# Perceiver layer on one core: half tiles shared by a pair of batches, probabilities left undivided with their inverses turned in DRAM, scores on other banks right behind the logits, softmax in parts

## The chip, the cores and the metric

The kernel runs on one core of one Trainium2 chip. The metric is the device time of one execution in microseconds. All data are float32.

## The reference

There are 32 batches with 64 latents x (128 features) and a context of 1,601 rows of 128 features. A mask selects for each batch at most 400 rows at the end of its context. Three residual blocks follow each other:

```python
# cross attention: 16 heads of 64; keys and values are the selected context rows and the 64 latents
q = ln(x) @ Wq * scale; k, v = split([ln(ctx), ln(x)] @ Wkv)
x = x + layernorm(softmax(mask(q @ k.T)) @ v @ Wout)
# self attention over the 64 latents: 16 heads of 8, a slope bias on the distance
x = x + softmax(q @ k.T / sqrt(8) + slopes * dist) @ v @ Wo + bo
# feed-forward: SiLU gate, 128 -> 352 -> 128, activations and weights rounded to 8 bits,
# with one scale over the maximum of all batches
x = x + ffn(layernorm(x))
```

## The kernel before, in words

The batches are sorted on the chip by how many context rows they need, and each place in the sorted order has a fixed cap (`CAPS`, line 26). If the caps do not hold, a switch (line 910) takes one of two wider versions; with these inputs the first, called narrow, runs. Two batches are worked on as a pair (t, u), u = 0 or 1: place t with place 31 - t (`batch`, line 182). A batch has 64 + cap columns of keys: one tile of 128 rows that holds the latents of one of the two and 64 context rows, then nt = (cap - 64) // 128 full tiles, then a rest. With the caps before, there is no rest.

The weights are folded ahead: a_sb is Wq times Wk for each head and b_sb is Wv times Wout, so a query has 128 features and is multiplied with the normalised context itself, whose rows also serve as values.

A pair has 8 steps, one for each couple c of heads. All 16 pairs make 128 steps. For each step and batch:

- `logits` (lines 553 to 585): one matmul of the queries with the turned context into bank_s (L568), at most 512 columns; VectorE adds the mask and takes the minimum of the negated logits (L571); ScalarE takes the exponential and sums it (L576). VectorE then inverts the sums (L582) and multiplies the probabilities with them (L585).
- `turned` (lines 587 to 619): two steps later TensorE transposes the probabilities tile by tile into bank_t (L604, L614), and ScalarE copies them out (L607, L615).
- `attend` (lines 621 to 640): after every second step TensorE multiplies context rows by turned probabilities for four heads, 256 columns a tile, into bank_m (L632), and VectorE copies the result out (L637).

After a pair's steps `project` (L663) applies b_sb over 16 heads, the layer norm follows, and the self-attention of the pair: `self_T` (L689), `self_qkv` (L700 to L722), `self_softmax` (scores L738, bias addition L750, maximum L754, subtraction L755, exponential L759), `self_pT`, `self_values` (L788), `self_out` (L804). Before a pair's steps `load` brings context rows and mask (L445 to L455) into one of three buffers, `prepare` normalises them (moments L494, then L502, L224, L225), `keys_T` turns them (L243), and `queries` (L544) multiplies latents by a_sb.

There are eight PSUM banks: two bank_s, three bank_t, three bank_m. The program is written as a list of steps: `at(step, f, ...)` enters a function under a step, and the last loop runs the logits of a step, then what stands under it. `chain` (lines 832 to 837) gives the steps after a pair's end at which the parts of its self-attention stand. A scheduler then orders the instructions of each engine; each engine and each DMA queue runs its own in order. All loads in the loop go through SP's queue.

After the loop the feed-forward part (lines 915 to 1029) needs the maximum over all batches first.

Of the kernel before, what the change touches and what calls it, by code (L numbers as in the profile page):

```python
# [25 lines left out]
CAPS = [448] * 9 + [320] * 8 + [192] * 7 + [64] * 8  # L26
# [11 lines left out]
def perceiver_layer(  # L38
# [16 lines left out]
    small = ctx.enter_context(tc.tile_pool(name="small", bufs=4))  # L55
    ps_s = ctx.enter_context(tc.tile_pool(name="ps_s", bufs=2, space=PSUM))
# [125 lines left out]
    def batch(t, u, engine=mybir.EngineType.SP, reorder=True, order=order):  # L182

        r = t if u == 0 else B - 1 - t
        _, (b,) = nc.values_load_multi_w_load_instructions(
            order[:, r : r + 1], engines=[engine], min_val=0, max_val=B - 1,
            skip_runtime_bounds_check_because="five bits of an integer", bass_reorder=reorder,
        )
        return b
# [196 lines left out]
    def attention(actx, name, caps):  # L386
# [4 lines left out]

        keep = actx.enter_context(tc.tile_pool(name=f"keep{name}", bufs=1))
# [3 lines left out]
        def cap(t, u):  # L396
            return caps[t if u == 0 else B - 1 - t]

        def shape(t, u):

            nt, rest = divmod(cap(t, u) - SL, P)
            return nt, rest, [P] * (1 + nt) + [rest] * (rest > 0), SL + cap(t, u)

        n_max = [max(len(shape(t, u)[2]) for t in range(NP)) for u in range(2)]
        k_max = [max(shape(t, u)[3] for t in range(NP)) for u in range(2)]
# [17 lines left out]
        for u in range(2):  # L423
            for x_ in xns[u]:
                nc.gpsimd.memset(x_[lat[u], 0, :], 0.0)
                if not narrow:
                    nc.gpsimd.memset(x_[:, n_max[u] - 1, :], 0.0)
            for a_ in addends[u]:
                nc.gpsimd.memset(a_[:, lat[u]], 0.0)
# [5 lines left out]
        masks, lns, lnTs, xTs, qTs, oTs, probs, pTs = {}, {}, {}, {}, {}, {}, {}, {}  # L435

        def load(t, u):
            r = xns[u][t % NX]
            nt, rest, _, _ = shape(t, u)
            first = S2 - cap(t, u)  # L440
            b = first_pair[u] if t == 0 else batch(t, u)
            if t and narrow:
                load_x(t, u, b)
            rows = context[bass.ds(b, 1)].rearrange("b s d -> (b s) d")
            nc.sync.dma_start(out=r[tok[u], 0, :], in_=rows[first : first + SL])  # L445
            lo = first + SL
            if nt:
                nc.sync.dma_start(
                    out=r[:, 1 : 1 + nt, :],
                    in_=rows[lo : lo + nt * P].rearrange("(p n) d -> p n d", n=nt),  # L450
                )
            if rest:
                nc.sync.dma_start(out=r[:rest, 1 + nt, :], in_=rows[S2 - rest :])
            m = two.tile([P, cap(t, u)], U8, tag=f"mask{u}", name=f"mask{t}_{u}")
            nc.sync.dma_start(  # L455
                out=m,
                in_=mask[bass.ds(b, 1)].rearrange("b s -> (b s)")[first:].partition_broadcast(P),
            )
            masks[t, u] = m
# [26 lines left out]
        def prepare(t, u):  # L486

            nt, rest, tiles, sk = shape(t, u)
            n_all = len(tiles)
# [11 lines left out]
            for n in range(n_all):  # L501
# [8 lines left out]
            nc.gpsimd.tensor_scalar(  # L510
                ad[:, tok[u]], m[:, :SL], BIG, -BIG, ALU.mult, ALU.add
            )
            if nt:
                nc.gpsimd.tensor_scalar(
                    ad[:, P : P + nt * P].rearrange("q (n p) -> q n p", p=P),
                    m[:, lo:hi].rearrange("q (p n) -> q n p", n=nt),
                    BIG, -BIG, ALU.mult, ALU.add,
                )
            if rest:
                nc.gpsimd.tensor_scalar(  # L520
                    ad[:, P + nt * P : sk], m[:, hi:], BIG, -BIG, ALU.mult, ALU.add
                )

        def keys_T(t, u):
            nt, rest, _, sk = shape(t, u)
            xn = xns[u][t % NX]
            xT = two.tile(
                [P, k_max[u]], FP, tag=f"xT{u}", name=f"xT{t}_{u}", bufs=2 if narrow else 1
            )
            view = xT[:, : (1 + nt) * P].rearrange("p (n c) -> p n c", c=P)  # L530
            for n in range(0, 1 + nt, 4):
                e = min(n + 4, 1 + nt)
                transposed(view[:, n:e, :], [xn[:, j, :] for j in range(n, e)], nc.scalar.copy)
            if rest:
                transposed(xT[:, (1 + nt) * P :].unsqueeze(1), [xn[:rest, 1 + nt, :]])
            xTs[t, u] = xT
# [16 lines left out]
        def logits(t, c, us):  # L553

            den = small.tile([P, len(us)], FP, tag=f"den{name}", name="den")
            for i, u in enumerate(us):
                sk = shape(t, u)[3]
                w = qTs[t][:, u, 2 * c : 2 * c + 2, :].rearrange("p h i -> p (h i)")
                s = two.tile(
                    [P, k_max[u]], FP, tag=f"s{u}" if narrow else "s", name=f"s{t}_{u}_{c}",  # L560
                    bufs=4 if narrow else 2,
                )[:, :sk]
# [3 lines left out]
                for j, (k, e) in enumerate(pieces):  # L566
                    ps = bank_s()
                    nc.tensor.matmul(  # L568
                        ps[:, : e - k], lhsT=w, rhs=xTs[t, u][:, k:e], start=True, stop=True
                    )  # L570
                    nc.vector.tensor_tensor_reduce(  # L571
                        out=s[:, k:e], in0=ps[:, : e - k], in1=addends[u][t % NA][:, k:e],
# [5 lines left out]
                    accum_out=den[:, i : i + 1],  # L578
                )
                probs[t, u, c] = s  # L580
            rden = small.tile([P, len(us)], FP, tag=f"rden{name}", name="rden")
            nc.vector.reciprocal(rden, den)  # L582
            for i, u in enumerate(us):
                s = probs[t, u, c]
                nc.vector.tensor_scalar_mul(s, s, rden[:, i : i + 1])  # L585

        def turned(t, c, u):

            nt, rest, tiles, _ = shape(t, u)
            n_all = len(tiles)  # L590
# [19 lines left out]
            for n in range(0, 1 + nt, 4):  # L610
                e = min(n + 4, 1 + nt)
                bt = bank_t().rearrange("p (j c) -> p j c", c=P)
                for j in range(n, e):
                    nc.tensor.transpose(bt[:, j - n, :], s[:, j * P : (j + 1) * P], ident)  # L614
                nc.scalar.copy(pT[:, n:e, odd, :], bt[:, : e - n, :])  # L615
            if rest:
                bt = bank_t()
                nc.tensor.transpose(bt[:rest, :P], s[:, (1 + nt) * P :], ident)
                evacuate(pT[:rest, 1 + nt, odd, :], bt[:rest, :P])

        def attend(t, c, u):
# [5 lines left out]
            pT = pTs.pop((t, u, c))  # L627
            po = bank_m()
            xn = xns[u][t % NX]
            tiles = shape(t, u)[2]  # L630
            for n, k in enumerate(tiles):
                nc.tensor.matmul(  # L632
                    po[:, : 2 * P], lhsT=xn[:k, n, :],
                    rhs=pT[:k, n].rearrange("p o c -> p (o c)"),
                    start=(n == 0), stop=(n == len(tiles) - 1),
                )
            nc.vector.tensor_copy(  # L637
                oTs[t][:, 2 * c : 2 * c + 4, u, :],
                po[:, : 2 * P].rearrange("p (h i) -> p h i", i=SL),
            )  # L640
# [17 lines left out]
        def project(t, part, parts=2):  # L658
# [8 lines left out]
            if part < parts - 1:  # L667
                return
            oTs.pop(t)
# [61 lines left out]
        def self_softmax(t):  # L731
            q, kx = own[t]

            ps = [bank_s(), bank_t(), bank_m(), bank_m()]
# [10 lines left out]
            stat = small.tile([P, H], FP, tag="stat", name="stat")  # L745
            for g in range(2):
                hs = slice(g * 8, g * 8 + 8)
                for r in (2 * g, 2 * g + 1):
                    hr = slice(4 * r, 4 * r + 4)
                    nc.vector.tensor_tensor(  # L750
                        p[:, hr], ps[r][:, : 4 * SL].rearrange("p (h k) -> p h k", k=SL),
                        bias[:, hr], ALU.add,
                    )
                nc.vector.tensor_reduce(stat[:, hs], p[:, hs], AX.X, ALU.max)  # L754
                nc.vector.tensor_tensor(  # L755
                    p[:, hs], p[:, hs],
                    stat[:, hs].unsqueeze(2).to_broadcast([P, 8, SL]), ALU.subtract,
                )
                nc.scalar.activation(p[:, hs], p[:, hs], AF.Exp)  # L759
            own[t] = p  # L760

# [40 lines left out]
        def self_out(t):  # L802
            po = bank_m()
            nc.tensor.matmul(po[:, :D], lhsT=own.pop(t), rhs=swT[:, 3, :], start=True, stop=True)  # L804
            nc.vector.tensor_tensor(x1[:, t, :], po[:, :D], x1[:, t, :], ALU.add)
            norm1(x3[:, t, :], x1[:, t, :])
# [23 lines left out]
        for t in range(NP):  # L830
            s0, e = CH * t, CH * (t + 1)
            if not narrow:
                chain = (4, 5, 9, 10, 12, 16, 17, 18, 19)
            elif t < NP - 2:
                chain = (4, 5, 7, 8, 10, 13, 14, 15, 16)
            else:
                chain = (None, None, 4, 5, 6, 8, 8, 9, 10)
# [6 lines left out]
            if t == NP - 1:  # L844
                for k in range(3):
                    at(e + chain[2], ffn_turn, k)
            for k, (f, *more) in zip(
                chain[2:],
                (
                    (self_T,), (self_qkv,), (self_softmax,), (self_pT, 0), (self_pT, 1),  # L850
                    (self_values,), (self_out,),
# [48 lines left out]
        for i in range(max(later) + 1):  # L900
            if i < len(steps):
                logits(*steps[i])
            for f, args in later.get(i, ()):
# [161 lines left out]
```

## Time and profile before

| | us |
|---|---|
| median of 3 runs (lowest, highest) | 691.11 (690.61, 691.83) |
| the profiled execution | 692.31 |
| its span | 690.3 |
| mean granted TensorE clock | 0.961 |
| PE busy / VectorE / ScalarE / GpSimd | 620.7 / 518.7 / 409.8 / 130.0 |
| PE idle before L568, released by VectorE's L750 / L571, whole span | 11.3 / 9.0 |
| start of the first and last logits record | 33.2 / 593.2 |

The profile is one execution, taken by the hardware. L568 is line 568 of the kernel. PE is TensorE's matmuls, PEld its weight loads, DVE VectorE, ACT ScalarE, POOL GpSimd, SP the engine that issues most DMAs. A row of a group gives line, engine, operation, output <- inputs, shape and count, then busy time and the mean ns of one, then the idle time of the engine just before the group and what released it. A row of a window gives the stretch, its length, the busy time (and instructions) of PE, PEld, DVE, ACT and POOL, the granted clock, the share of DMA time and GB/s. A row of a wait gives total us, times, longest. A row of the chain gives start, length and what the chain of waits followed there. A DMA row ends with the median time from issue to landing.

### The profile page before, as it was taken

The page shows a single profiled execution, that of the slowest core. Times are in us where ns is not written, and L with a number is a line of the kernel's source. Part 1 is how long each engine was busy: PE and PEld are TensorE (multiplying, and loading weights), DVE is VectorE, ACT ScalarE, POOL GpSimd, SP SyncE. Part 2 cuts the span into 40 slices and gives each one's busy share as a digit, 9 for nine tenths or more (in the row PEclk, how much of TensorE's full clock was granted, in tenths as well). Part 3 has the DMA queues.
Part 4 walks back from the last instruction along what each step waited for, and adds up shares of the span by engine and source line. Part 5 has one row for each costly group of instructions (what it writes and reads, how often), then busy time and mean ns, then how long its engine had stood idle before and what let it go on. Part 6 is the DMA issues. An engine that isn't in the chain of part 4 may idle for free.

```text
span 690.3 us, 14206 instructions
## 1 busy us (share of the span) xinstructions
PE 620.7 (90%) x4798; PEld 496.9 (72%) x4798; DVE 518.7 (75%) x1992; ACT 409.8 (59%) x1096; POOL 130.0 (19%) x273
## 2 busy tenths in 40 slices
PE   4598999999998989898999999999999999954975
PEld 3576878777786868686878888888887886843335
DVE  4487777787868797878778888888888778644673
ACT  2386667666675766675766767676766566512441
POOL 1338320211111112121111212020202000010002
PEclk9599999999999999999999999999999999975988
DMA  4520100000001010100000010000000000000002
GB/s 103 118 56 0 25 1 24 2 24 1 24 2 23 2 30 1 24 1 20 5 11 14 11 15 8 18 7 19 5 24 1 1 1 1 1 1 3 1 0 62
DMA packets 20580, 11.98 MB, mean 17 GB/s; under 512 B 7748, under 2 KB 20036, under 8 KB 20500
## 3 DMA queue, kind: packets, MB, share of 16 engines
q1 hardware_dynamic: 19476, 10.02, 6.4%
q10 hardware_dynamic: 864, 0.82, 0.4%
q8 instruction: 40, 0.66, 0.4%
q14 instruction: 40, 0.33, 0.2%
q0 software_dynamic: 160, 0.16, 0.1%
HBM read 9.94 MB, written 1.05 MB: 16 GB/s over the span
## 4 chain that ended last, share of the span: by engine, by line
PE 49%; DVE 26%; ACT 8%; POOL 5%; issue 5%; DMA 2%; SPq 0%; POOLq 0%; DVEq 0%; ACTq 0%
PE bank_m L632 11%; PE bank_s L568 10%; PE bank_m L663 6%; PE bank_m L544 5%; ACT s L576 5%; DVE s L571 5%; POOL rstd L469 5%; DVE s L585 5%; PE bank_t L614 4%; PE bank_s L971 3%; PE bank_t L243 3%; DVE oT L637 2%; PE bank_m L998 2%; PE bank_t L604 2%; PE bank_m L788 1%
## 5 line engine op out<-in xcount | busy, mean ns | idle before, releaser
L576 ACT ACTIVATE s<-s,low 128x512 f32<-128x512 f32 (+3 forms) x256 | 143.8, 563 | 100.7 <-DVE low L571 87.5
L568 PE MATMUL bank_s<-xT,qT 128*128 128x512 f32 (+3 forms) x512 | 170.6, 449 | 20.6 <-DVE p L750 11.3
L632 PE MATMUL bank_m<-pT,xn 128*128 128x256 f32 x656 | 166.6, 381 | 1.6 <-ACT pT L615 1.4
L568 PEld LDWEIGHTS bank_s<-xT,qT 128*128 128x128 f32 x512 | 88.5, 194 | 77.8 <-DVE p L750 21.5
L469 POOL TENSOR_TENSOR rstd<-rstd,mhalf 128x1 f32<-128x1 f32 (+2 forms) x96 | 61.1, 638 | 411.7 <-DVE rstd L465 387.3
L632 PEld LDWEIGHTS bank_m<-pT,xn 128*128 128x128 f32 x656 | 118.2, 190 | 18.8 <-ACT pT L615 3.4
L571 DVE CUSTOM_DVE_ANT_0 s<-bank_s,ad 128x512 f32<-128x512 f32 (+3 forms) x256 | 121.0, 486 | 8.7 <-PE bank_s L568 7.9
L615 ACT COPY pT<-bank_t 128x512 f32<-128x512 f32 (+1 forms) x136 | 70.4, 523 | 51.5 <-PE bank_t L614 51.3
L585 DVE TENSOR_SCALAR s<-s,rden 128x512 f32<-128x512 f32 (+3 forms) x256 | 89.6, 391 | 2.0
L614 PE MATMUL bank_t<-ident,s 128*128 128x128 f32 x480 | 75.3, 273 | 0.0
L544 PE MATMUL bank_m<-lnT,a_sb 128*128 128x128 f32 x512 | 70.8, 284 | 0.4 <-ACT lnT L244 0.4
L614 PEld LDWEIGHTS bank_t<-ident,s 128*128 128x128 f32 x480 | 60.6, 141 | 13.6 <-issue 1.0
L544 PEld LDWEIGHTS bank_m<-lnT,a_sb 128*128 128x128 f32 x512 | 65.4, 201 | 0.7 <-ACT lnT L244 0.7
L663 PE MATMUL bank_m<-b_sb,oT 128*128 128x128 f32 x512 | 63.3, 276 | 0.5 <-DVE oT L637 0.5
L663 PEld LDWEIGHTS bank_m<-b_sb,oT 128*128 128x128 f32 x512 | 60.0, 192 | 1.7 <-DVE oT L637 1.3
L637 DVE COPY oT<-bank_m 128x256 f32<-128x256 f32 x128 | 53.2, 415 | 10.5 <-PE bank_m L632 10.2
L502 ACT ACTIVATE xn<-xn,shift,rstd 128x128 f32<-128x128 f32 x82 | 36.6, 490 | 25.5 <-DVE shift L498 25.4
L576 ACT ACTIVATION_READ_ACCUMULATOR s<-s,low 128x1 f32 x256 | 48.4, 189 | 0.0
L548 ACT COPY qT<-bank_m 128x512 f32<-128x512 f32 x64 | 37.4, 584 | 16.2 <-PE bank_m L544 15.8
L582 DVE RECIPROCAL rden<-den 128x2 f32<-128x2 f32 x128 | 20.4, 159 | 30.2 <-ACT s L576 29.4
L604 PE MATMUL bank_t<-ident,s 128*128 128x128 f32 x176 | 29.0, 273 | 0.0
L607 ACT COPY pT<-bank_t 128x256 f32<-128x256 f32 (+1 forms) x60 | 28.0, 466 | 0.0
(179 smaller groups left out, 853.5 us busy)
## 6 DMA issues: line engine op xcount, KB each, us to landing
xn<-in_ctx_dram SPq DMA_DIRECT2D x9, 192.0 KB, 2.4
x<-in_x_dram SPq DMA_DIRECT2D x32, 32.0 KB, 2.3
xn<-in_ctx_dram SPq DMA_DIRECT2D x32, 32.0 KB, 2.0
xn<-in_ctx_dram SPq DMA_DIRECT2D x8, 128.0 KB, 2.0
out_dram<-y SPq DMA_DIRECT2D x18, 32.0 KB, 1.9
wk_sb<-in_L_xattn_Wkv_dram ACTq DMA_DIRECT2D x1, 512.0 KB, 4.2
wq_sb<-in_L_xattn_Wq_dram SPq DMA_DIRECT2D x1, 512.0 KB, 5.1
wv_sb<-in_L_xattn_Wkv_dram SPq DMA_DIRECT2D x1, 512.0 KB, 5.3
```

Source lines behind the costliest of these rows:

```text
L469: nc.gpsimd.tensor_tensor(rstd, rstd, mhalf[:, :n], ALU.pow)
L544: nc.tensor.matmul(pm[:, j * P : (j + 1) * P], lhsT=a_sb[:, h4 + j, :], rhs=lnTs[t], start=True, stop=True,)
L568: nc.tensor.matmul(ps[:, : e - k], lhsT=w, rhs=xTs[t, u][:, k:e], start=True, stop=True)
L571: nc.vector.tensor_tensor_reduce(out=s[:, k:e], in0=ps[:, : e - k], in1=addends[u][t % NA][:, k:e], scale=-1.0, scalar=3e38 if j == 0 else ...
L576: nc.scalar.activation(s, s, AF.Exp, bias=low[:, len(pieces) - 1 :], scale=-1.0, accum_out=den[:, i : i + 1],)
L585: nc.vector.tensor_scalar_mul(s, s, rden[:, i : i + 1])
L604: nc.tensor.transpose(bt[:, n, o, :], s[:, n * P : (n + 1) * P], ident)
L614: nc.tensor.transpose(bt[:, j - n, :], s[:, j * P : (j + 1) * P], ident)
L615: nc.scalar.copy(pT[:, n:e, odd, :], bt[:, : e - n, :])
L632: nc.tensor.matmul(po[:, : 2 * P], lhsT=xn[:k, n, :], rhs=pT[:k, n].rearrange("p o c -> p (o c)"), start=(n == 0), stop=(n == len(tiles) - 1),
L637: nc.vector.tensor_copy(oTs[t][:, 2 * c : 2 * c + 4, u, :], po[:, : 2 * P].rearrange("p (h i) -> p h i", i=SL),)
L663: nc.tensor.matmul(pm[:, :D], lhsT=oT[:, h].rearrange("p u i -> p (u i)"), rhs=b_sb[:, h, :], start=(h == 0), stop=(h == H - 1),)
```

## The change

1. **Caps and pairs.** The caps come in steps of 64 and are tighter; the pairs are a written list. A rest is now 0 or 64, the same for both of a pair, and the rests of both lie in one tile: rows 0 to 63 are batch 0's, 64 to 127 batch 1's. The probabilities of both batches lie next to each other, so that this tile is turned by one transpose; its attend matmul is done once for each batch, on half the rows.
2. **Undivided probabilities.** The multiplication L585 goes. The sums of two steps and both batches are inverted together (4 columns). SP writes them, turned, to a small tile in DRAM, and reads that back as one row of 512 values for all 128 partitions. The copy L637 becomes a product with that row.
3. **Scores.** `self_softmax` is split into `self_scores` (the matmuls, and the bias additions) and two halves of the softmax at their own steps. The scores take two bank_t and two bank_m instead of one bank_s, one bank_t and two bank_m, and stand first under their step, right behind the logits.
4. **Norms** that stood inside `project` and `self_out` are functions with steps of their own.

```diff
-CAPS = [448] * 9 + [320] * 8 + [192] * 7 + [64] * 8
+CAPS = [448] * 4 + [384] * 5 + [320] * 2 + [256] * 6 + [192] * 6 + [128] + [64] * 8
+PAIRS = [
+    (17, 31), (4, 15), (0, 24), (5, 14), (18, 30), (6, 13), (1, 25), (19, 22),
+    (7, 12), (2, 26), (16, 23), (8, 11), (3, 27), (20, 21), (9, 28), (10, 29),
+]
...
+    dram = ctx.enter_context(tc.tile_pool(name="dram", bufs=4, space=bass.MemoryType.DRAM))
...
-        r = t if u == 0 else B - 1 - t
+        r = PAIRS[t][u]
...
         def logits(t, c, us):
...
+            odd, n_us = c % 2, len(us)
+            if not odd:
+                sums[t, us[0]] = small.tile([P, 2 * n_us], FP, tag=f"den{name}", name="den")
+            den = sums[t, us[0]]
+            both = two.tile(
+                [P, s_max], FP, tag="s", name=f"s{t}_{us[0]}_{c}", bufs=4 if narrow else 2
+            )
...
-            rden = small.tile([P, len(us)], FP, tag=f"rden{name}", name="rden")
-            nc.vector.reciprocal(rden, den)
-            for i, u in enumerate(us):
-                s = probs[t, u, c]
-                nc.vector.tensor_scalar_mul(s, s, rden[:, i : i + 1])
+            if odd:
+                nc.vector.reciprocal(den, den)
+                line = dram.tile([2 * n_us, P], FP, tag=f"line{name}", name="line")
+                nc.sync.dma_start(out=line.rearrange("j p -> p j"), in_=den)
+                rden = two.tile(
+                    [P, 2 * n_us * P], FP, tag="rden", name=f"rden{t}_{us[0]}_{c}",
+                    bufs=3 if narrow else 2,
+                )
+                nc.sync.dma_start(
+                    out=rden, in_=line.rearrange("j p -> (j p)").partition_broadcast(P)
+                )
+                view = rden.rearrange("d (o u h i) -> d u o h i", h=2, o=2, u=n_us)
+                for i, u in enumerate(us):
+                    sums[t, u, c - 1] = view[:, i]
...
         def attend(t, c, u):
...
-            nc.vector.tensor_copy(
-                oTs[t][:, 2 * c : 2 * c + 4, u, :],
-                po[:, : 2 * P].rearrange("p (h i) -> p h i", i=SL),
-            )
+            if rest and narrow and u == 0:
+                return
+            both = (0, 1) if rest and narrow else (u,)
+            if rest:
+                for v in both:
+                    i, n, on = rest_of(t, v)
+                    nc.tensor.matmul(
+                        open_[v][:, : 2 * P], lhsT=xns[i][t % NX][on, n, :],
+                        rhs=pTs[t, i, c][on, n].rearrange("p o c -> p (o c)"),
+                        start=False, stop=True,
+                    )
+            for v in both:
+                nc.vector.tensor_tensor(
+                    oTs[t][:, 2 * c : 2 * c + 4, v, :].rearrange("p (o h) i -> p o h i", o=2),
+                    open_.pop(v)[:, : 2 * P].rearrange("p (o h i) -> p o h i", o=2, h=2),
+                    sums.pop((t, v, c)), ALU.mult,
+                )
...
-        def self_softmax(t):
+        def self_scores(t):
...
-            ps = [bank_s(), bank_t(), bank_m(), bank_m()]
+            ps = [bank_t(), bank_t(), bank_m(), bank_m()]
...
-                chain = (4, 5, 7, 8, 10, 13, 14, 15, 16)
+                chain = (5, 5, 6, 7, 8, 10, 11, 12, 13, 14, 15, 16, 17)
...
-                chain = (None, None, 4, 5, 6, 8, 8, 9, 10)
+                chain = (None, None, 3, 4, 5, 6, 6, 6, 8, 8, 9, 10, 10)
...
-            for f, args in later.get(i, ()):
+            for f, args in sorted(later.get(i, ()), key=lambda x: x[0] is not self_scores):
                 f(*args)
```

## The prediction

> **What bounds the kernel now.** I read the page's shares first, then the slices, then the busy time of a long stretch, then who waited for whom on PE in that stretch, then the chain that ended last.
>
> ```profile
> PE 620.7 (90%) x4798; PEld 496.9 (72%) x4798; DVE 518.7 (75%) x1992; ACT 409.8 (59%) x1096; POOL 130.0 (19%) x273
> ...
> PEclk9599999999999999999999999999999999975988
> ...
> 50.00:590.00 540.00, 517.57 (x4101) 423.09 (x4100) 431.97 (x1718) 353.69 (x979) 108.58 (x211) 1.00 0.05 11
> ```
>
> The third line is the pair loop: 540 us long, PE busy 517.6 of them at a granted clock of 1.00, DVE 432.0, ACT 353.7. So PE is the bound there and has 22.4 us of idle; the other 150 us of the span are set-up, the tail of the attention and the feed-forward part, which the change leaves alone. The waits of PE in the same stretch name the idle:
>
> ```profile
> PE bank_s L568 <- DVE p L750: 11.3, 12, 1.3
> PE bank_s L568 <- DVE low L571: 8.5, 9, 1.8
> PE bank_m L632 <- ACT pT L615: 1.4, 4, 0.4
> ```
>
> The logits' bank is held by the self-attention's scores (first line), or the logits run ahead of VectorE (second). Whether PE is really full or only looks so is told by the chain of waits, where PE stands uncovered piece after piece:
>
> ```profile
> 327.54 0.87 PE bank_m L632 x4
> 328.41 1.29 PE bank_s L568 x4
> 329.70 0.86 PE bank_m L632 x4
> 330.56 0.44 PE bank_t L614 x4
> 331.00 1.79 PE bank_m L663 x16
> ```
>
> An fp32 matmul leaves two records, a transpose one. Columns per piece: L568 is 2 records of 512 and 2 of 256, 1,536 columns in 1.29 us; L632 is 4 x 256 = 1,024 in 0.86; L614 4 x 128 in 0.44. All give 0.84 to 0.86 ns a column. That is the price I use for PE work: PE streams, and only columns or waits taken away shorten the loop.
>
> **The change part by part.**
>
> *Half tiles and new pairs.* The caps sum to 8,448 before and 7,680 after; with 64 latents for each of 32 batches, 10,496 columns against 9,728, or 82 tiles of 128 against 76. The instruction order of the changed kernel has the same 256 logits matmuls, with 77,824 columns where there were 83,968: 6,144 fewer, two records each, 12,288. Probability transposes go from 656 to 608 (48 x 128 = 6,144 columns), key transposes from 82 to 76 (768). Together 19,200 columns x 0.84 = **-16.1 us** on the bounding engine. The attend matmuls stay 328 of 256 columns: a shared tile is multiplied twice, by 64 rows each.
>
> *Those 48 half matmuls* (24 neighbouring couples, on rows 0-63 and 64-127) may run side by side. The nearest row is the scores, four row groups:
>
> ```profile
> 321.58 0.43 PE L738 MATMUL bank_m<-kx,q 32*64 32x256 f32 x2
> 321.85 0.38 PE L738 MATMUL bank_m<-kx,q 32*64 32x256 f32 x2
> 322.19 0.33 PE L243 MATMUL bank_t<-ident,ln 128*128 128x128 f32 x1
> ```
>
> There 16 records of 256 columns start within 0.30 us and the next transpose 0.62 us after the first; one after the other they would take 16 x 0.215 = 3.4 us. So tiles do overlap. The Trainium skill (TensorEngine Tiling (Array Packing), Key Properties) says against it that changing the tiling mode drains the engine. Four records cost 0.86 us in sequence; side by side 0.43, plus a drain, for which the scores leave 0.62 - 0.43 = 0.19 us. By the overlap alone 24 x 0.43 = 10 us are won, with the drain 24 x 0.24 = 6, and without any overlap the drain loses 24 x 0.19 = 5. I take **-3**, ends -10 and +5.
>
> *Undivided probabilities.* This takes VectorE work away:
>
> ```profile
> L585 DVE TENSOR_SCALAR s<-s,rden 128x512 f32<-128x512 f32 x72 | 35.6, 495 | 0.9
> L637 DVE COPY oT<-bank_m 128x256 f32<-128x256 f32 x128 | 53.2, 415 | 10.5 <-PE bank_m L632 10.2
> L750 DVE TENSOR_TENSOR p<-bank_m,bias 128x256 f32<-128x256 f32 x32 | 13.2, 413 | 0.0
> ```
>
> All four forms of L585 are 89.6 us; 64 reciprocals of 128 go (10.2); the copy of 415 ns becomes a product of a PSUM bank and an SBUF tile of the same size, which L750 does in 413 ns: nothing. L571 costs (676-278)/384 = 1.04 ns a column, x 6,144 = 6.4. VectorE loses about 106 us plus 4 for six tiles of normalisation, so it falls from 518.7 us of the span to some 409. ScalarE loses 5.4 in the exponentials (0.87 ns a column) and about 7 in the copies. None of this is on PE, so it is worth only what it takes out of PE's waits: of the 8.5 us behind L571 I take 3.5 away (ends 0 and 8.5).
>
> *Scores on other banks.* The logits no longer share a bank with the scores, and the four additions come before any maximum. The 11.3 us go. What is late next: the scores now hold two of three bank_t and two of three bank_m until four additions at some 0.33 us are done. In PE's new order about 2 us of attend and logits work lie between the scores and the next instruction that needs a held bank, against about 1.3 us of additions plus what VectorE has in front. I leave 3 us (about 0.2 us x 16; ends 0 and 16). Net **-8** here, **-3.5** above. Cutting the softmax into parts adds no instruction.
>
> *The inverses through DRAM.* Added on SP's queue: 64 times a write of 512 single fp32 elements, and 64 reads of 256 KB that wait for it. Nothing before looks like that write. Nearest rows, issue to landing:
>
> ```profile
> xn<-in_ctx_dram SPq DMA_DIRECT2D x9, 192.0 KB, 2.4
> mask<-in_mask_BxS_bk_dram SPq DMA_DIRECT2D x9, 56.0 KB, 3.0
> sbk_c<-in_L_attn_bk_dram SPq DMA_DIRECT2D x1, 0.5 KB, 3.1
> clip<-in_L_ffn_clip_x_dram SPq DMA_DIRECT2D x1, 0.5 KB, 3.6
> ```
>
> The sbk_c row is 128 elements of 4 bytes (its twin sbq_c took 4.5, but in the set-up, where the DMA engines were 60% busy against 5% in the loop). If 512 cost no more, the write takes 3.1; if every further 128 elements add the 1.1 us by which 128 short rows lie above a 64-row load (2.0), it takes 3.1 + 3 x 1.1 = 6.4. The Trainium skill (DMA: Bandwidth & Descriptors, Rules for kernel authors) speaks against this part: a strided last dimension becomes one descriptor per element; and the page's fixed cost of about 2 us is mostly the receipt of the write, longest for HBM. By the page alone an estimate is 2 us plus something; by the rows 3.1 to 6.4. I take 4.5. The read is near the 192 KB row: 3. With two issues of about 0.5 us, inverse to landing is 4.5 + 0.5 + 3 + 0.3 = **8.3 us**.
>
> Who waits: the product on VectorE, and behind it the logits' L571 and so PE. In the changed order the product stands three or four steps behind its reciprocal in all but three of 64 cases. 128 steps in some 525 us are 4.1 us each, so three are 12.3. For the lightest pairs (384 columns, two of 16) I estimate 5 x 384 x 0.84 ns plus about 1.4 us of shared work = 3.0 us a step, 9.1 for three. It is covered, barely in those. Cost zero, and if the cover is gone, each us missing costs up to 64 us.
>
> SP is moved past too. Each write-read couple blocks it for 4.5 + 0.5 us, and the loads of the pair after next queue between:
>
> ```profile
> SPq L445 <- PE bank_m L632: 386.1, 25, 30.4
> ```
>
> Before, SP spent 386 us waiting for a free context buffer, so there is time; but the loads now start some us later and VectorE's moments of that pair wait for them (3.2 us before). VectorE would be idle for over a third of the loop ((432 - 108) / 525 busy), so I count nothing of that, ends 0 and 12.
>
> *Head and tail.* The first pair has 3 tiles where it had 5: **-1**. The last pair's final product waits for two transfers: 8.3 us after the last reciprocal, where before the last copy came 10.8 us after it (598.2 to 608.9), and the work between shrinks by some 2 to 3 us: **+1** (ends 0 and 5).
>
> Sum: -16.1 - 3 - 8 - 3.5 - 1 + 1 = -30.6. The profiled execution took 692.31 us (span 690.3 and 2.0 around it), so 661.7; the median of the runs is 1.2 lower, so **660.5**.
>
> **The rivals.**
>
> 1. *PE work and waits shrink as summed* (chance 0.64): 660.5, from 648 (L571's waits, the drain and the held banks all at their good ends) to 671.
>
> 2. *The transfers are just late* (0.20): the write lands at about 6 us, light steps and loads behind it hold VectorE by about 2 us in a third of 64 cases, or the held banks cost their full 13 more. 15 us of the gain are lost: 675. For: three steps are only 12 us. Against: VectorE has slack, and two bank_s banks lie between it and PE.
>
> 3. *SP's queue becomes the bound* (0.12), slower than before: write, wait, read and loads go in order. One period is the write's landing L, 0.5 for the read's issue and about 0.9 for a quarter of a pair's loads. The loop before is 557 us, or 8.7 per period of 64, so it decides from L = 7.3 us; at 7.5 the loop is 64 x 8.9 = 570 and the execution about 705. For: no row shows 512 small writes. Against: the rows end at 6.4.
>
> 4. *Nothing is left of it* (0.04): 691, when the held banks and late loads give back some 30 us.
>
> 0.2% of 691, 1.4 us, is about what a measurement of this kernel can tell from no change. Faster: 0.64 + 0.19 + 0.01; within: 0.03; slower: 0.13. The range reaches from 648 to rival 2's far side, 684.
>
> **What would show it.** PE busy should be about 601, L568's columns 155,648, and L585 gone. PE's waits for p L750's successor should be near 3 us. The write's landing time is the number that decides: below 6 us the first case holds; above 7.3 the third, with VectorE idle before the product, released by a DMA. If the half matmuls' records do not overlap, 3 to 8 us are missing.

## The result, and the profile after

The changed kernel takes **890.92 us** (median of 4 runs, 880.99 to 891.43), the kernel before 691.40 beside it (4 runs): ratio 1.285, 95% interval 1.276 to 1.294. The prediction, 660.5 us and faster, was wrong, and 890.92 lies above its range (648 to 684). The profiled execution took 891.43 us, its span is 889.8.

From the page: busy time, the granted clock in 40 slices, and the DMA issues with the median from issue to landing at the end of the row.

```profile
PE 669.6 (75%) x4744; PEld 522.2 (59%) x4744; DVE 436.4 (49%) x1666; ACT 398.5 (45%) x1070; POOL 128.4 (14%) x287
...
PEclk8777788989889898979899898979797898886697
...
rden<-line SPq DMA_DIRECT2D x64, 256.0 KB, 4.6
xn<-in_ctx_dram SPq DMA_DIRECT2D x44, 32.0 KB, 3.3
line<-den SPq DMA_DIRECT2D x64, 2.0 KB, 9.7
```

VectorE's busy time falls by 82 us (518.7 to 436.4), yet PE, the bounding engine, is busy for longer than before and idle for a quarter of the span. The row `line<-den`, the write of the inverses, had been taken at 4.5 us and lands in 9.7. The chain of waits follows the same transfer:

```profile
PE 34%; DMA 31%; DVE 7%; SPq 3%; issue 2%; ACT 2%; POOL 1%; DVEq 0%; ACTq 0%; POOLq 0%
```

Now the loop, from the first to the last logits record: first before, then after (columns as explained ahead of the prediction).

```profile
33.20:593.20 560.00, 537.08 (x4226) 436.99 (x4226) 447.22 (x1789) 368.08 (x1018) 113.90 (x221) 1.00 0.05 13
```

```profile
32.60:779.70 747.10, 582.83 (x4181) 460.81 (x4180) 366.21 (x1470) 357.25 (x994) 113.14 (x233) 0.89 0.25 31
```

The loop holds 187 of the span's 199.5 us of loss; the tail behind it takes 110.1 us where it took 97.1. In the loop PE idle rises from 23 to 164 us (747.1 - 582.8), and PE busy rises by 46 although there is less to stream, at a granted clock of 0.89. Who waits, in the kernel after (SP over the whole span, the others from 50 to 800 us; total us, times, longest):

```profile
SPq L635 <- DMA line<-den: 555.0, 64, 11.3
...
DVE st L522 <- DMA xn<-in_ctx_dram: 131.0, 21, 10.4
DVE oT L712 <- DMA rden<-line: 78.8, 20, 7.7
...
PE bank_s L612 <- DVE low L615: 108.5, 23, 10.1
PE bank_m L695 <- DVE oT L712: 18.4, 7, 6.2
```

SP stands 555 us before the read (L635) until the write has landed. VectorE waits in two places: at the first moments of new context rows (L522), and at the product (L712). PE waits for VectorE's L615 behind either. One such stretch, first on SP's queue:

```profile
322.15 0.39 SPq L630 DMA_DIRECT2D line<-den  x1
332.58 0.32 SPq L635 DMA_DIRECT2D rden<-line  x1
333.17 0.47 SPq L473 DMA_DIRECT2D xn<-in_ctx_dram  x1
...
336.65 0.53 SPq L630 DMA_DIRECT2D line<-den  x1
```

then on VectorE, and on PE (the bracket is the idle time before the instruction and its releaser):

```profile
337.60 0.59 DVE L522 BATCH_NORM_STATS2 st<-xn 128x6 f32<-128x128 f32 x2 [8.29 <-DMA xn<-in_ctx_dram]
```

```profile
339.31 2.50 PE L612 MATMUL bank_s<-xT,qT 128*128 128x512 f32 x4 [5.03 <-DVE low L615]
...
353.75 1.25 PE L612 MATMUL bank_s<-xT,qT 128*128 128x512 f32 x4
```

The read waits 10 us for the write, the context load behind it goes out only at 333.17, VectorE sits idle for 8.29 us for those rows, and PE behind it for 5.03. The logits that follow stream at half speed: 2.50 us at a granted clock of 0.50 (339.31 to 341.81) for what takes 1.25 us at 1.00 from 353.75. So one late transfer is paid twice on PE. The Trainium skill (TensorE: Matmul & The Clock Gate, HAM oscillation) has the rule: idle gaps of PE above about 3.4 us throttle the array again. This stretch, with its gap of 5.03 us, agrees; the last section has one that does not.

### The profile page after: what moved, and what is told of

It reads as the page before. It is cut to its first block, busy times and chain, and to the rows that moved or that the text cites. A ratio compares the mean times of both kernels' runs of the same rounds, so it can differ in the third digit from the quotient of the medians.

```text
span 889.8 us, 14107 instructions
## 1 busy us (share of the span) xinstructions
PE 669.6 (75%) x4744; PEld 522.2 (59%) x4744; DVE 436.4 (49%) x1666; ACT 398.5 (45%) x1070; POOL 128.4 (14%) x287
## 4 chain that ended last, share of the span: by engine, by line
PE 34%; DMA 31%; DVE 7%; SPq 3%; issue 2%; ACT 2%; POOL 1%; DVEq 0%; ACTq 0%; POOLq 0%
DMA line<-den 18%; PE bank_s L612 7%; DMA rden<-line 6%; PE bank_m L695 6%; DMA xn<-in_ctx_dram 4%; PE bank_m L740 4%; PE bank_m L580 3%; PE bank_s L1056 2%; PE bank_t L669 2%; DMA mask<-in_mask_BxS_bk_dram 2%; PE bank_t L249 2%; PE bank_m L1083 1%; DVE s L615 1%; PE bank_t L659 1%; PE bank_m L869 1%
## 5 line engine op out<-in xcount | busy, mean ns | idle before, releaser
L612 PE MATMUL bank_s<-xT,qT 128*128 128x128 f32 (+6 forms) x512 | 178.1, 474 | 110.6 <-DVE low L615 110.5
L620 ACT ACTIVATE s<-s,low 128x128 f32<-128x128 f32 (+6 forms) x256 | 138.1, 541 | 202.3 <-DVE low L615 156.7
L498 POOL TENSOR_TENSOR rstd<-rstd,mhalf 128x1 f32<-128x1 f32 (+3 forms) x96 | 59.0, 622 | 570.9 <-DVE rstd L494 489.7
L695 PEld LDWEIGHTS bank_m<-pT,xn 128*128 128x128 f32 x560 | 108.7, 206 | 51.5 <-DVE oT L712 15.1
L615 DVE CUSTOM_DVE_ANT_0 s<-bank_s,ad 128x128 f32<-128x128 f32 (+6 forms) x256 | 111.6, 465 | 26.1 <-PE bank_s L612 22.8
L712 DVE TENSOR_TENSOR oT<-bank_m,rden 128x256 f32<-128x256 f32 x128 | 52.3, 417 | 96.0 <-DMA rden<-line 84.0
L522 DVE BATCH_NORM_STATS2 st<-xn 128x6 f32<-128x128 f32 x76 | 20.1, 278 | 134.6 <-DMA xn<-in_ctx_dram 134.0
L740 PE MATMUL bank_m<-b_sb,oT 128*128 128x128 f32 x512 | 66.0, 289 | 15.5 <-ACT qT L584 10.1
L580 PEld LDWEIGHTS bank_m<-lnT,a_sb 128*128 128x128 f32 x512 | 68.4, 207 | 11.9 <-DVE ws L363 3.8
L740 PEld LDWEIGHTS bank_m<-b_sb,oT 128*128 128x128 f32 x512 | 63.8, 205 | 18.3 <-ACT qT L584 10.5
L681 ACT COPY pT<-bank_t 128x512 f32<-128x512 f32 (+1 forms) x96 | 52.4, 546 | 23.3 <-PE bank_t L669 13.9
L669 PEld LDWEIGHTS bank_t<-ident,s 128*128 128x128 f32 x312 | 41.0, 150 | 18.3 <-issue 10.1
L841 ACT ACTIVATE p<-p 128x512 f32<-128x512 f32 x32 | 20.0, 629 | 60.7 <-DVE p L838 60.6
L662 ACT COPY pT<-bank_t 128x512 f32<-128x512 f32 (+1 forms) x80 | 37.4, 484 | 1.5 <-PE bank_t L659 1.5
```

The costliest lines, as they stand in the source:

```text
L498: nc.gpsimd.tensor_tensor(rstd, rstd, mhalf[:, :n], ALU.pow)
L580: nc.tensor.matmul(pm[:, j * P : (j + 1) * P], lhsT=a_sb[:, h4 + j, :], rhs=lnTs[t], start=True, stop=True,)
L612: nc.tensor.matmul(ps[:, : e - k], lhsT=w, rhs=xTs[t, u][:, lo + k : lo + e], start=True, stop=True)
L615: nc.vector.tensor_tensor_reduce(out=s[:, k:e], in0=ps[:, : e - k], in1=addends[u][t % NA][:, lo + k : lo + e], scale=-1.0, scalar=3e38 if ...
L620: nc.scalar.activation(s, s, AF.Exp, bias=low[:, len(pieces) - 1 :], scale=-1.0, accum_out=den[:, odd * n_us + i : odd * n_us + i + 1],)
L662: nc.scalar.copy(pT[:, :n_all], bt)
```

## The experiments

Theory S at the start: SP's queue, blocked for the write's landing once per period, paces the loop. Its rivals: the latency from inverse to landed read (some 15 us: 9.7 for the write, 4.6 for the read, two issues) is longer than the three steps it has (L), and the pairs or the scores also cost time.

**Part 2 undone** (`e1_divided`): parts 1, 3 and 4 stay.

```diff
-            if odd:
-                nc.vector.reciprocal(den, den)
...
+            nc.vector.reciprocal(rden, den)
+            for i, s in enumerate(parts):
+                nc.vector.tensor_scalar_mul(s, s, rden[:, i : i + 1])
...
-                nc.vector.tensor_tensor(
+                nc.vector.tensor_copy(
```

> The changed kernel with only its second part undone: probabilities are divided on VectorE again, the bank is copied out again, no write to and read from DRAM. Half tiles, pairs, scores on other banks and the softmax in parts stay. Theory Q (the write of 512 single elements on SP's queue causes the whole loss): about 665 us, from 655 to 680, PE busy near 602. Rival B (banks held by the scores, half tiles or the new order of the softmax cause a good part of the loss): over 700 us.

Measured: 678.77 us, ratio 0.981 (0.979 to 0.983). Without the transfers the kernel is faster than before, so the whole loss stands in part 2.

**Part 2 alone** on the kernel before (`e2_only_turn`).

> The kernel before with the second part alone: undivided probabilities, sums of two steps inverted together, written turned to DRAM and read back. Old caps, old pairs, old scores. Theory Q: the period of SP's queue sets the loop whatever the other parts do, so about the changed kernel's time, 870 to 910 us. Rival B: under 800 us.

Measured: 974.41 us, ratio 1.408 (1.405 to 1.412), above the 870 to 910 expected. The write lands in 11.1 us here, and the product waits 212.9 us for the read, the rows' moments 79.0 for their load. With parts 1, 3 and 4 beside it, in the changed kernel, the time is 83 us lower; which of them makes part 2 cost less is not shown.

**The write in the tile's own layout** (`e3_plain_line`): 128 runs of 16 bytes; the product steps over the row instead.

```diff
-                line = dram.tile([2 * n_us, P], FP, ...)
-                nc.sync.dma_start(out=line.rearrange("j p -> p j"), in_=den)
+                line = dram.tile([P, 2 * n_us], FP, ...)
+                nc.sync.dma_start(out=line, in_=den)
...
-                view = rden.rearrange("d (o u h i) -> d u o h i", h=2, o=2, u=n_us)
+                view = rden.rearrange("d (h i o u) -> d u o h i", h=2, o=2, u=n_us)
```

> The changed kernel with the small tile in DRAM laid out as the sums lie in SBUF (128 rows of 4), so that the write is 128 runs of 16 bytes in place of 512 of 4; the read stays one row of 512 values for all partitions, and the product reads it with a step of 4. Same bytes, same queue, same waits. Theory Q1 (the time of the write goes with its number of runs): the write lands in about 4 us (2 us and a quarter of 7.7), SP's queue has room, 660 to 675 us. Rival Q2 (a write to DRAM followed by a read of it is slow whatever its shape): the write lands in 8 to 10 us and the time stays over 850.

Measured: **672.09 us**, ratio 0.970 (0.968 to 0.973), faster than before and than the kernel of the first experiment. Rows of its page, a group and its loop:

```profile
rden<-line SPq DMA_DIRECT2D x64, 256.0 KB, 3.8
...
line<-den SPq DMA_DIRECT2D x64, 2.0 KB, 1.8
```

```profile
L712 DVE TENSOR_TENSOR oT<-bank_m,rden 128x256 f32<-128x256 f32 x128 | 78.2, 619 | 14.6 <-PE bank_m L695 7.6 <-PE bank_m L706 6.5
```

```profile
33.90:571.60 537.70, 521.85 (x4181) 423.99 (x4180) 386.19 (x1470) 355.85 (x994) 112.92 (x232) 0.99 0.21 43
```

The same 2 KB, the same queue, the same order: the write lands in 1.8 us where it took 9.7, the product no longer waits for a DMA, and the clock is back at 0.99. Against this loop the one after is 209 us longer with the same 4,181 PE records: 148 us of idle (164.3 against 15.9) and 61 us of matmuls at a lower clock. The price is the product's operand in steps of four elements, 619 ns where it was 417 (52.3 us in all, in the kernel after), on an engine that has room.

**The write from ScalarE's queue** (`e4_act_write`).

```diff
-                nc.sync.dma_start(out=line.rearrange("j p -> p j"), in_=den)
+                nc.scalar.dma_start(out=line.rearrange("j p -> p j"), in_=den)
```

> The changed kernel with the write of the inverses issued from ScalarE's queue; the read stays on SP. The landing of the write stays at 9 to 10 us, so inverse to product is as long as before, but SP's queue no longer waits from issue to landing of each write in turn with its loads: the next write can be under way. Theory S (the serial queue sets the pace): the time falls by over 80 us, to 720 to 800. Rival L (the latency from inverse to product, about 15 us against three steps, sets the pace by itself): within 30 us of the changed kernel's 890.

Measured: 855.45 us in the faster of two runs; the other, 872.81, is the one profiled. Theory S's number is missed, and the faster run lies just outside L's. SP still stands 575 us before the reads, and the loads behind them wait as before. Moving the write brings some 35 us of the 80 and more expected while its reader sits in the loads' queue.

**The attend two steps later** (`e5_later_attend`), with one more buffer of turned probabilities and of the rows of inverses; `far` is true in the version that runs.

```diff
-                    at(i + 3 + (u if narrow else 0), attend, t, c - 1, u)
+                    at(i + (5 if far else 3) + (u if narrow else 0), attend, t, c - 1, u)
```

> The changed kernel with its slow write, but every attend, and the product in it, stands two steps later (five or six steps behind the second logits of its couple in place of three or four), and the self-attention's parts two steps later with it; three buffers of turned probabilities and four of the inverses where there were two and three. Nothing else moves. Theory L (the latency from inverse to product, 15 us against three or four steps, sets the pace): VectorE's waits for the read, 84 us, vanish and the time falls by some 60 to 120 us, to 770 to 830. Theory Q (SP, blocked until each write has landed, sets the pace through its own period or through the loads behind it): 870 to 900, VectorE waits as long, only for other things.

Measured: 890.34 us (2 runs), nothing gained: L as the only limit falls. The product's wait over the whole span goes from 84 to 26 us, but the wait for context rows grows to 182.5.

**Loads from ScalarE's queue** (`e8_loads_act`), from the third pair on; the other loads of a pair likewise.

```diff
-            nc.sync.dma_start(out=r[tok[u], 0, :], in_=rows[first : first + SL])
+            eng.dma_start(out=r[tok[u], 0, :], in_=rows[first : first + SL])
```

> The changed kernel with the loads of the loop (latents, context rows, mask from the third pair on) issued from ScalarE's queue; the writes and reads of the inverses stay alone on SP's. The write lands as late as before. Theory Q, second half (context loads held behind the writes on SP's queue are what VectorE waits for): the 134 us of waits for context rows go and the time falls by 80 us or more, to about 800. If the period of SP's writes and reads alone is the bound (64 periods of 9.7 + 0.5 us and what the next inverse adds, some 10.5 to 11 us each, against 11.7 now): 820 to 860. Theory L: 870 to 900.

Measured: 864.32 us, ratio 1.251 (1.247 to 1.255). SP now holds nothing but writes and reads, and a write still starts only every 11.5 us: 10.5 to land, and about 1 between. The loads, with no wait for the read before them, land late all the same:

```profile
xn<-in_ctx_dram ACTq DMA_DIRECT2D x38, 32.0 KB, 5.6
```

That is 5.6 us against 3.3 after and 2.1 with part 2 undone. The traces show what these loads meet. Of the kernel after's loads, the landing can be told for 70. The 16 that were issued while a write was under way all landed behind that write, 6.5 to 10.9 us after their issue; the other 54 took at most 5.4. With the loads on ScalarE's queue it can be told for nine, all issued during a write, and all nine again landed behind it, after 4.4 to 10.1 us. So a load that meets the write waits for it on either queue. The Trainium skill (DMA: Bandwidth & Descriptors, Issuing engines are not separate DMA queues) states that transfers run on the same 16 DMA engines whichever engine issues them, and that another issuer saves only the time of issuing. These landings agree with it, though the engines were far from full (a busy share of 0.25 in the loop after).

**Twice as many elements** (`e6_double_write`): 1,024, in eight rows; the read takes the first four.

```diff
-                line = dram.tile([2 * n_us, P], FP, ...)
-                nc.sync.dma_start(out=line.rearrange("j p -> p j"), in_=den)
+                line = dram.tile([4 * n_us, P], FP, ...)
...
+                nc.vector.tensor_copy(den2[:, : 2 * n_us], den)
+                nc.vector.tensor_copy(den2[:, 2 * n_us :], den)
+                nc.sync.dma_start(out=line.rearrange("j p -> p j"), in_=den2)
```

> The changed kernel with the write doubled: the four columns of inverses are copied twice side by side and all eight columns are written, 1,024 single elements; the read takes the first 512 as before. If the time of the write goes with its number of elements: 2 + 2 x 7.7 = 17 us to landing, and with a period of about 19.2 us the time is about 64 x 19.2 + 133 = 1,360 us. If it is a fixed cost of a write that is read back: still 10 us and about 900.

Measured: 931.07 us (2 runs), ratio 1.348 (1.343 to 1.352); this write lands in 9.6 us (the median of the few landings that can be told). SP's wait before a read is 9.6 us on average (583.0 in 61) where it was 8.7 (555.0 in 64), and a write starts every 12.6 us where it was 11.9, which makes the 40 us more (63 x 0.65). So twice the elements cost about 1 us and not 7.7, and a price per element falls as the explanation.

**Shapes of the write, alone** (`e10_write_shapes`): the plain-line kernel, with 18 more writes behind its end, each waiting for the one before.

```diff
+            "wfourrows": ([4, P], lambda d: d.rearrange("j p -> p j"), 4),
+            "wonerow": ([1, P], lambda d: d.rearrange("j p -> p j"), 1),
+            "weightrows": ([8, P], lambda d: d.rearrange("j p -> p j"), 8),
+            "wfar": ([P, 4, 16], lambda d: d[:, :, 0], 4),
+            "wplain": ([P, 4], lambda d: d, 4),
+            "wapart": ([P, 128], lambda d: d[:, :4], 4),
```

> The plain-line version with 18 added writes to DRAM behind its last stores, one after another on SP's queue (each waits until the one before has landed, by way of a small copy on GpSimd), nothing else running: six shapes three times. Only their landing is read; the kernel gets longer by them. Fourrows: 512 single elements, four rows of 512 bytes, as in the change. Onerow: 128 elements into one row. Eightrows: 1,024 into eight rows. Far: 512 elements 64 bytes apart. Plain: 128 runs of 16 bytes in one piece. Apart: 128 runs of 16 bytes, 512 bytes apart. Theory N (number of runs): onerow 3 to 4 us, fourrows 9 to 10, eightrows 17, far 9 to 10, plain and apart 2 to 3. Theory B (4-byte writes of many partitions into the same 512 bytes hold each other up, rows side by side): onerow, fourrows and eightrows all 8 to 11, far below 5, plain and apart 2 to 3.

Measured, issue to landing:

```profile
wfourrows<-q SPq DMA_DIRECT2D x3, 2.0 KB, 8.4
wonerow<-q SPq DMA_DIRECT2D x3, 0.5 KB, 7.2
weightrows<-q SPq DMA_DIRECT2D x3, 4.0 KB, 9.6
...
wfar<-q SPq DMA_DIRECT2D x3, 2.0 KB, 2.5
wplain<-q SPq DMA_DIRECT2D x3, 2.0 KB, 1.4
wapart<-q SPq DMA_DIRECT2D x3, 2.0 KB, 1.4
```

`wfar` has the 512 single elements of `wfourrows`, 64 bytes apart in DRAM, and lands in 2.5 us, so neither the number of runs nor their 4 bytes is dear by itself. `wplain` puts the runs of 32 partitions into each 512 bytes and lands in 1.4, so neighbours are not dear by themselves either. Dear are the two together: single elements of many partitions next to each other. `wonerow` has only 128 of them, in one row of 512 bytes, and takes 7.2. Runs of 8 bytes and distances between 4 and 64 were not tried. Rows proceed nearly side by side: four cost 1.2 us more than one by these medians, and between 1 and 3 by the starts of the copies that wait for them.

The trace also tells where in the landing the time lies. One `wonerow`, issued at 675.82 and landed at 683.03, in two windows:

```profile
675.80:676.90 1.10, 0.00 (x0) 0.00 (x0) 0.00 (x0) 0.00 (x0) 0.00 (x0) 0.50 0.07 1
676.90:683.00 6.10, 0.00 (x0) 0.00 (x0) 0.00 (x0) 0.00 (x0) 0.00 (x0) 0.50 0.00 0
```

Its packets are on the DMA engines in the first 1.1 us alone (a share of 0.07). In the 6.1 us after that the share is 0.00 and nothing has landed. So the long part lies between the last packet and the landing; what passes there no view shows.

**Write on ScalarE's queue and a later attend** (`e9_act_later`), **then the loads there too** (`e12_all_three`): two and then all three of the edits to queues and steps above, together.

> The two experiments that changed little alone, together: the slow write is issued from ScalarE's queue, and the attend and the product stand two steps later. Then no write waits behind a read on SP, and the latency of some 15 us from inverse to landed read lies under five or six steps. If period and latency each hold the loop at nearly the same pace, so that undoing one shows the other: below 800 us. If the loads behind the reads on SP, which still wait for each write, are enough by themselves: 840 to 880.

> The changed kernel with three moves at once: the write of the inverses and, from the third pair on, the loads of the loop go to ScalarE's queue, and the attend stands two steps later. SP's queue is left with the reads alone. Theory (three limits near the same pace: the period of write and read on one queue, the 15 us of latency under three steps, the loads held behind the reads): with all three taken away the loop goes back towards PE's own pace, 680 to 740 us, VectorE's waits for the context rows and the product's wait for the read both under 30 us, and the granted clock back above 0.95. Rival (the write of 512 elements takes 9.7 us of a resource that all transfers share, so moving it between queues doesn't help): the writes still come no closer than 10 to 11 us, 800 us or more, whichever queue they stand on. A third case, the loads on ScalarE's queue hold its exponentials while they wait for a free buffer: 740 to 800, with ScalarE idle before an exponential behind a load.

Measured: 820.37 us (819.52 and 821.22), and for all three 792.58 and 800.06 us (809.28 in a third run; ratio 1.151, 1.142 to 1.161). Each relief helps a little, but the first number falls between the two expected, and three separate limits as the whole explanation fall with the second. The rival's sign is there: a write starts only every 10.4 us. The third case's is there in part: ScalarE's exponentials wait 34.6 us for loads. With the product's wait down to 8.9 us, VectorE still waits for context rows in the last kernel (50 to 700 us):

```profile
DVE st L527 <- DMA xn<-in_ctx_dram: 127.8, 31, 9.4
```

There the loads stand behind the write on ScalarE's queue; on SP's they stand behind the read that waits for it. No placement tried took the write off their way, which fits the landings above. How the loss divides among queue, latency and loads behind the write is open. What is shown is that a write of 1.8 us ends all of it.

**The pairs alone** (`e7_pairs_only`) and **the scores and parts of the softmax alone** (`e11_scores_only`) on the kernel before.

> The kernel before with the first part alone: the new caps and pairs and the shared half tiles; probabilities divided on VectorE, scores, softmax and norms where they were. By the prediction's sum: -16.1 for columns, -3 for half matmuls side by side, -1 at the head, so about 671 from 691. If the measured gain of the divided version (678.8) came from half tiles alone, 679 here too; if the half tiles are worth what was summed and the other scores cost time, below 679.

> The kernel before with the third and fourth part alone: scores on two bank_t and two bank_m right behind the logits, softmax in parts, norms with steps of their own. Old caps and pairs, probabilities divided. By the prediction's sum -8 us: 683. Pairs alone gave 702 and both together 679: if the two add up, 668 here; if the new scores only mend what the new pairs break, 685 to 692.

Measured: 702.26 us, ratio 1.015 (1.010 to 1.020), and 689.93 us, 0.998 (0.997 to 1.000). The second is hardly clear of noise. The pairs alone lose time although they stream less, which none of the three cases expected. PE's waits from 50 to 570 us in that kernel, and its loop:

```profile
PE bank_s L610 <- DVE p L814: 14.5, 13, 1.6
PE bank_s L610 <- DVE low L613: 7.2, 8, 1.6
PE bank_m L683 <- ACT qT L584: 5.0, 3, 3.5
```

```profile
32.70:607.00 574.30, 540.96 (x4191) 428.80 (x4190) 438.52 (x1790) 357.63 (x995) 115.30 (x233) 0.99 0.05 12
```

The loop is 14.3 us longer than before: 10.4 us more idle, and 3.9 more busy where nearly the same matmuls took 527.7 us in the kernel with part 2 undone. The wait for the scores' bank, the first line, is 3.2 us longer than before and the wait for queries, the third, is new. Of the busy time, three stretches at a granted clock of 0.50 (17.0 us from 79.1, 184.9 and 485.3) cost 8.5. With the scores on other banks the time falls by 23.5 us from the pairs alone, while the scores alone bring 1.3. So the scores mend what the pairs break, and the parts of this change do not add. Why the pairs alone wait more and lose the clock is not shown in full.

## Why the prediction was wrong

**The step that failed** is "I take 4.5" for the write, with ends at 3.1 and 6.4. It measured 9.7 in the kernel, 8.4 alone. The rows it was sized from were reads of short runs, and the upper end added a price for each further 128 elements. The runs show another cost: adjacent single elements from many partitions, for which a write waits some 6 us after its last packet. With 9.7 for the write and 4.6 for the read, where 3 was taken, inverse to landed read is some 15 us against 8.3, and no longer covered by the 12.3 us of three steps. The Trainium skill's rule (DMA: Bandwidth & Descriptors, Rules for kernel authors), one descriptor per element for a strided last dimension, warned in the right place for another reason: `wfar` keeps its 512 elements and lands in 2.5 us. Its page also gives 512 bytes as the least transfer for the full rate, and says that smaller ones are read, modified and written (Specifications). That alone is not the cost either: runs of 16 bytes landed in 1.4 us.

**Rival 3** came nearest to what happened. Its point, L = 7.3 us, was passed, and its sum with L = 9.7 gives 64 x 11.1 = 710 for the loop and 845 for the execution. Measured: writes issued from 37.2 to 789.2, 63 periods of 11.9 us. So the transfer, the direction and SP's wait for it were right, its chance of 0.12 too low, and its sum 46 us short. The queue alone is not the whole path, though. SP also stood 72 us before its writes waiting for VectorE, and with write and loads on the other queue and the product later, 100 us and more of the loss remain. The rival also left out that the clock falls in the gaps, 61 us more PE busy than in the plain-line kernel. How the 46 us divide among these is not shown.

**"I count nothing"** for late loads (ends 0 and 12) failed too: 131 us of VectorE's waits are for context rows. SP's old wait of 386 us was indeed free time, but a load behind a wait of 10 us starts when the wait ends, not when a buffer is free, and one behind the write lands after it.

**The rest, read from the plain-line kernel**, where the transfers are covered: span -19.8 us against the -30.6 of the sum.

| step | predicted | measured |
|---|---|---|
| columns and half matmuls (PE busy in the loop) | -16.1 - 3 | -15.2 |
| PE's waits in the loop | -8 - 3.5 | -7.1 |
| head, tail | -1, +1 | +0.7, +1.8 |

PE busy of the whole span is 605.0, with 601 foretold. VectorE's busy time was to fall to some 409 us and fell to 436.4 in the kernel after: the groups that went measured what was said, but a sum of groups doesn't see that neighbouring records overlap. The good ends named for the range's 648 (L571's waits, the half matmuls, the held banks) add up to 645.5. The half matmuls do overlap: in the kernel after, four records take 0.63 us from their start to the next instruction's (297.96 to 298.59), where 0.86 would be in sequence, and the attends of the first experiment fall by 4.3 us (166.6 to 162.3). The logits' wait for VectorE is 4.5 us from 8.5, as said, and the scores' wait is 0.4 where 3 were left. What is new in its place are waits that the prediction didn't list, 3.4 us for queries from ScalarE and 3.1 before L566 that nothing in the profile explains. The product in the place of the copy cost nothing, as said: 417 ns for 415.

So part 2 done well gains little over part 2 undone, 672.09 against 678.77 us: VectorE's 50 us less of busy time were hardly on the path. Of the plain-line kernel's 20.6 us against the kernel before beside it (692.64), 13.9 come from the parts other than part 2.

## What to carry to other kernels

Size a small turned write to DRAM by where its elements land: write in the layout that the tile has and let the reader take the stride, on the engine with slack. Here single elements side by side cost 6 to 8 us more than runs of 16 bytes. A write and a read that waits for it, on the queue of the loads, cost a landing time per period and hold the loads as well, and a load that meets the slow write on another queue still lands behind it; when the bounding engine then waits in gaps of some us, add what the clock loses. Try parts of a change in pairs before calling one useless: here the pairs lost 1.5% alone and the scores changed next to nothing (0.2%), together they won 1.9%.

## What the runs showed of the hardware

- 128 single elements from 128 partitions into 512 bytes of DRAM landed in 7.2 us, with packets on the DMA engines in the first 1.1 us alone; 512 of them 64 bytes apart landed in 2.5, and 128 runs of 16 bytes in 1.4.
- In the kernel after, 16 loads issued on the write's own queue while it was under way, and nine on the other queue in the kernel with the loads moved, all landed behind the write, up to 10.9 us after their issue.
- A VectorE product of 128 x 256 took 619 ns with an SBUF operand in steps of four elements, 417 with one in sequence.
- In the kernel with the pairs alone the granted clock fell to 0.53 from 184.6 to 190.0 us, though PE's longest idle in the 30 us ahead was 1.21 us; in this stretch no gap of some us was needed for it.
